# Lighter router and statistics, norms per tile, a fixed ring of contexts, two shared blocks in the transition, and text order from there on

## The chip, the cores and the metric

The kernel runs on one core of a Trainium2 chip. The metric is the device time of one execution in microseconds (us), the median of several runs; beside it stands one profiled execution, whose trace is what every reading here rests on. The engines are TensorE (PE, with its weight loads shown as PEld), VectorE (DVE), ScalarE (ACT), GpSimd (POOL) and SyncE (SP, which here issues DMAs).

## The reference

A block of cross attention is followed by a mixture of experts, all in fp32, on 32 sequences of 100 tokens with 256 features; each sequence has a context of 361 rows with 192 features.

```
x1 = layernorm(layernorm(x)); x2 = layernorm(ctx)           # affine forms of both
q, k, v = x1 Wq + bq, x2 Wk + bk, x2 Wv + bv                # E = 256, one head
x = x + softmax(q k^T / sqrt(E)) v Wo + bo
n = layernorm(x)
shared = gelu(n ws1 + bs1) ws2 + bs2                        # 256 -> 256 -> 256
aff = softmax(n Wr + br)                                    # 31 experts
gates = the 3 largest of aff, else 0
routed = sum over e of gates_e * (gelu(n We1_e + Be1_e) We2_e + Be2_e)
x = x + (shared + routed + n)
```

## The kernel before

The 3200 tokens are 25 tiles of 128, held in SBUF for the whole run as seven blocks `xb[k]` of up to four tiles. The work has four stages.

**Attention** loops over the 32 sequences (a batch each). Wq, Wk and Wv, Wo are folded into two matrices beforehand, so that one iteration transposes the context of batch i (`ctx_transpose`), computes the scores of batch i-1 (`scores`: the maximum on DVE, the exponential on ACT), and transposes and weighs batch i-2 (`exp_transpose`, `weighted`, which copies to a ring `cT`). When 128 tokens are done, `project_out` adds the result to the tile and takes its mean and variance. Contexts come in groups of GB = 4 batches: each has three chunks of rows, whose statistics are 12 `bn_stats` and 12 `bn_aggr`, followed by one `rsqrt` per group. That function is a root on ACT, a reciprocal on DVE and four DVE instructions of a Newton step; each root loads its own table on ACT, and so does the next exponential. The tile norms wait in the same way for `norms()`, once in four batches.

**Routing** is a pipeline through five functions of a tile, one step per iteration: `route_norm` normalises and transposes a tile, `route_gates` computes the logits, the three largest and a mask of the chosen experts, `route_slots` turns prefix counts (a running `base`, so that the tiles follow each other) into row numbers and scatters the tile's rows three times to `xs_d` in DRAM with indirect DMAs on POOL, `route_transpose` and `route_biases` add the gated second biases to the tile. POOL also adds the normalised tile to the tile itself (L500).

**The transition** derives from the counts which expert each of the 92 tiles of gathered rows belongs to, which takes a chain of small DVE instructions and a few transposes, and fetches rows and weights. The first shared block (`shared_first(0)`, `shared_second(0)`) is placed after it.

**The experts**: `run` handles 92 tiles; at step i it calls `turn(i)` (two transposes), `first(i-2)` (eight matmuls of We1, gelu on ACT) and `second(i-4)` (four matmuls of We2, a scaling, and a scatter to `y_d`). `fetch(q)` loads four tiles' rows and weights two groups ahead, `sort_out(q)` computes their gates and row numbers.

**The tail**: the other six shared blocks, and for each tile a read of its three rows from `y_d` (L929, four buffers), a sum on POOL (L931) and two on DVE (L932, L933), then one store per block.

A planner with a cost model orders the instructions of every engine; the text gives priorities and dependences. At run time each engine then works through its list in order, and each DMA queue its own.

Of the kernel before, what the change touches and what calls it, by code (L numbers as in the profile page):

```python
# [16 lines left out]
PSUM = bass.MemoryType.PSUM  # L17

# [16 lines left out]
def xattn_ffn(  # L35
# [27 lines left out]
    CODE, IX, GT, XW = D1, D1 + 1, D1 + 4, D1 + 8  # L63
    assert NS <= P and T % P == 0 and NE <= 32
# [14 lines left out]
    zpool = att_ctx.enter_context(tc.tile_pool(name="zpool", bufs=2 * GB + 2))  # L79
# [18 lines left out]

    ztile = {}

    def load_ctx(b):
        z = zpool.tile([P, NCH, DA], F32, tag="z", name=f"z_{b}")
        full = sum(1 for _, n in CH if n == P)
        nc.sync.dma_start(
            z[:, :full, :D2], ctx_in[b, : full * P, :].rearrange("(c p) d -> p c d", p=P)
        )
        for c in range(full, NCH):
            s, n = CH[c]
            nc.sync.dma_start(z[:n, c, :D2], ctx_in[b, s : s + n, :])
        nc.gpsimd.memset(z[:, :, D2:DA], 1.0)  # L110
        ztile[b] = z
# [35 lines left out]
    b2r = const.tile([NG, D1], F32, tag="b2r", name="b2r")  # L147
    nc.scalar.dma_start(b2r[:NE, :], Be2)
    nc.scalar.dma_start(b2r[NE:NG, :], bs2[None, :])
# [86 lines left out]
    for c in range(2):  # L236
# [6 lines left out]
        nc.vector.tensor_copy(m_sb[:, c, :], pm[:, :DA])  # L243
    AUG = [(0, 0, P), (1, P, A2)]
    c_sb = att.tile([P, 2], F32, tag="c", name="c_sb")
    for c, s, m in AUG:
# [6 lines left out]
        nc.vector.tensor_copy(c_sb[:m, c : c + 1], pc[:m, :1])  # L253
# [28 lines left out]
    def rsqrt(mv, n, mul, add, tag, name):  # L282

        v, s, y, r = (
            small.tile([P, n], F32, tag=f"{tag}{q}", name=f"{q}_{name}", bufs=3) for q in "vsyr"
        )
        nc.vector.tensor_scalar(v, mv[:, :, 1], mul, add, ALU.mult, ALU.add)
        nc.scalar.activation(s, v, AF.Sqrt)
        nc.vector.reciprocal(y, s)
        nc.vector.tensor_tensor(s, y, y, ALU.mult)  # L290
        nc.vector.tensor_tensor(s, s, v, ALU.mult)
        nc.vector.tensor_scalar(s, s, -0.5, 1.5, ALU.mult, ALU.add)
        nc.vector.tensor_tensor(r, y, s, ALU.mult)
        return r

# [3 lines left out]
    mvc, rc = {}, {}  # L299

    def ctx_stats_open(g):
        mvc[g] = small.tile([P, GB * NCH, 2], F32, tag="mvc", name=f"mvc_{g}", bufs=2)
        nc.gpsimd.memset(mvc[g], 1.0)

    def ctx_stats(b):
        g, i = divmod(b, GB)
        for c, (_, n) in enumerate(CH):
            stats(ztile[b][:n, c, :D2], mvc[g][:n, i * NCH + c, :], f"c{b}_{c}")

    def ctx_rsqrt(g):  # L310
        rc[g] = rsqrt(mvc[g], GB * NCH, 1.0, EPS, "c", f"c{g}")
# [8 lines left out]
    r1 = rsqrt(mv1, NT, 1.0 + EPS, EPS * EPS, "x", "x")  # L320
# [42 lines left out]
    def ctx_normalise(b):  # L363
        g, i = divmod(b, GB)
        z = ztile[b]
        for c, (_, n) in enumerate(CH):
            u = i * NCH + c
            normalise(z[:n, c, :D2], z[:n, c, :D2], mvc[g][:n, u, 0:1], rc[g][:n, u : u + 1])
# [14 lines left out]
    def scores(b):  # L383
# [7 lines left out]
        mx = small.tile([P, 1], F32, tag="mx", name=f"mx_{b}")  # L391
        nc.vector.tensor_reduce(mx[:L1, :], pss[:L1, :L2], AX.X, ALU.max)
        nm = small.tile([P, 1], F32, tag="nm", name=f"nm_{b}")
        nc.vector.tensor_scalar(nm[:L1, :], mx[:L1, :], -SC, None, ALU.mult)
        ex = work.tile([P, L2], F32, tag="ex", name=f"ex_{b}")
        nc.scalar.activation(ex[:L1, :], pss[:L1, :L2], AF.Exp, bias=nm[:L1, :], scale=SC)
# [16 lines left out]
    def weighted(b):  # L413
        z, exT = ztile.pop(b), att_eT.pop(b)
        for a, s, m in AUG:
# [6 lines left out]
            while q < L1:  # L422
                col = (b * L1 + q) % RING
                n = min(L1 - q, RING - col)
                if a == 0:
                    nc.scalar.copy(cT[:m, a, col : col + n], pw[:m, q : q + n])
                else:
                    nc.vector.tensor_copy(cT[:m, a, col : col + n], pw[:m, q : q + n])
# [3 lines left out]
    mv2 = {}  # L432

    def project_out(t, i, mv):
# [10 lines left out]
        stats(xt, mv[:, i, :], f"m{t}")  # L445

    xT = [qk[:, :, tiles[0] * P : (tiles[0] + len(tiles)) * P] for tiles in BLOCKS]
    GR = 4
    gates = const.tile([P, GR, NG], F32, tag="gates", name="gates")
    nc.gpsimd.memset(gates[:, :, NE:NG], 1.0)  # L450
# [43 lines left out]

    def route_norm(t):
# [4 lines left out]
        nc.gpsimd.tensor_tensor(xt, xt, xl, ALU.add)  # L500
        nc.gpsimd.tensor_scalar(row[:, CODE : CODE + 1], iota_3p, float(KTOP * P * t), None, ALU.add)
        nc.gpsimd.memset(row[:, XW - 1 : XW], 0.0)
# [6 lines left out]
    def route_gates(t):  # L509
# [16 lines left out]
        nc.vector.tensor_scalar(ix, i8[:, :KTOP], 1.0, None, ALU.add)  # L526
        mk = small.tile([P, NE], BF16, tag="mk", name=f"mk_{t}")
        nc.vector.tensor_scalar(mk, iota1, ix[:, 0:1], None, ALU.is_equal)
        for q in range(1, KTOP):
            nc.vector.scalar_tensor_tensor(mk, iota1, ix[:, q : q + 1], mk, ALU.is_equal, ALU.add)  # L530
# [4 lines left out]
        nc.vector.scalar_tensor_tensor(gates[:, t % GR, :NE], mk, rs, er, ALU.mult, ALU.mult)  # L535
        nc.scalar.activation(rows[t][:, GT : GT + KTOP], e3, AF.Copy, scale=rs)
        routing[t] = (mk, ix)

    def route_slots(t):

        mk, ix = routing.pop(t)
# [8 lines left out]
        sl = small.tile([P, KTOP], F32, tag="sl", name=f"sl_{t}")  # L550
        junk = small.tile([P, NE], F32, tag="junk", name=f"junk_{t}")
        for q in range(KTOP):
            nc.vector.scalar_tensor_tensor(
                junk, iota1, ix[:, q : q + 1], pos, ALU.is_equal, ALU.mult, accum_out=sl[:, q : q + 1]
            )
        su = small.tile([P, KTOP], U32, tag="su", name=f"su_{t}", bufs=6)
        nc.vector.tensor_copy(su, sl)
# [4 lines left out]
    def route_transpose(t):  # L562
        pg = ps_t(f"pg_{t}")
        nc.tensor.transpose(pg[:NG, :P], gates[:, t % GR, :], ident)
        gT[t] = small.tile([NG, P], F32, tag="gT", name=f"gT_{t}")
        nc.scalar.copy(gT[t], pg[:NG, :P])

    def route_biases(t):

        xt, _, _ = tile_of(t)  # L570
# [402 lines left out]
```

## Time and profile before

| | us |
|---|---|
| median of 3 runs | 577.51 (577.25 to 581.39) |
| profiled execution | 576.57 |
| its span, first to last instruction | 574.75 |
| last tile statistic of attention ends | 280.4 |
| last xs_d row numbers ready | 308.2 |
| first expert transpose | 325.26 |
| last expert scatter issued | 515.16 |
| first read of y_d issued | 520.22 |
| last DVE instruction ends | 568.91 |

| engine | busy us | share of the span |
|---|---|---|
| PE | 488.5 | 85% |
| DVE | 364.7 | 63% |
| ACT | 221.2 | 38% |
| POOL | 220.7 | 38% |

Busy shares are means over stages with different limits; a stage is read from its own window. The mean granted clock of PE is 0.918 of full speed. DMA moved 98.8 MB.

### The profile page before, as it was taken

The page shows a single profiled execution, that of the slowest core. Times are in us where ns is not written, and L with a number is a line of the kernel's source. Part 1 is how long each engine was busy: PE and PEld are TensorE (multiplying, and loading weights), DVE is VectorE, ACT ScalarE, POOL GpSimd, SP SyncE. Part 2 cuts the span into 40 slices and gives each one's busy share as a digit, 9 for nine tenths or more (in the row PEclk, how much of TensorE's full clock was granted, in tenths as well). Part 3 has the DMA queues.
Part 4 walks back from the last instruction along what each step waited for, and adds up shares of the span by engine and source line. Part 5 has one row for each costly group of instructions (what it writes and reads, how often), then busy time and mean ns, then how long its engine had stood idle before and what let it go on. Part 6 is the DMA issues. An engine that isn't in the chain of part 4 may idle for free. (4 is left out here: it accounts for less than half of the span.)

```text
span 574.8 us, 10701 instructions
## 1 busy us (share of the span) xinstructions
PE 488.5 (85%) x2798; PEld 387.9 (67%) x2798; DVE 364.7 (63%) x1737; ACT 221.2 (38%) x594; POOL 220.7 (38%) x334
## 2 busy tenths in 40 slices
PE   1649989888978979799665999999999999986892
PEld 1535757565656656577442699999999999973661
DVE  5497987997867989999876333433443343315663
ACT  0004463735426363736432244444444444431010
POOL 2000011443433344446675044444445444553432
PEclk9978988996968999999855899999999999999896
DMA  8892981221212131101222888888888888626975
GB/s 247 255 355 77 305 279 40 84 79 58 87 48 69 49 110 35 54 33 58 76 72 99 264 240 268 264 266 250 259 265 264 256 258 266 195 76 197 313 243 162
DMA packets 67634, 98.77 MB, mean 172 GB/s; under 512 B 8236, under 2 KB 43028, under 8 KB 67572
## 3 DMA queue, kind: packets, MB, share of 16 engines
q1 hardware_dynamic: 54880, 71.53, 41.9%
q0 software_dynamic: 8016, 22.21, 10.3%
q10 hardware_dynamic: 4676, 4.32, 2.3%
q8 instruction: 26, 0.43, 0.3%
q14 instruction: 36, 0.29, 0.2%
HBM read 68.22 MB, written 29.80 MB: 171 GB/s over the span
## 5 line engine op out<-in xcount | busy, mean ns | idle before, releaser
L456 POOL DMA_INDIRECT y_d<-ys,yrow x92 | 88.3, 959 | 115.2 <-DVE ys L874 72.5
L456 POOL DMA_INDIRECT xs_d<-xl,su x75 | 76.6, 1022 | 79.4 <-issue 14.8
L851 PE MATMUL ph<-xgT,w 128*128 128x128 f32 x736 | 101.6, 281 | 0.0
L856 ACT ACTIVATE hT<-ph,b1t 128x128 f32<-128x128 f32 x184 | 57.6, 364 | 101.7 <-PE ph L851 101.7
L851 PEld LDWEIGHTS ph<-xgT,w 128*128 128x128 f32 x736 | 94.8, 197 | 0.1
L866 PE MATMUL py<-w2r,hT 128*128 x368 | 94.3, 380 | 0.0
L866 PEld LDWEIGHTS py<-w2r,hT 128*128 128x128 f32 x368 | 62.9, 190 | 4.8
L418 PE MATMUL pcx<-exT,z 128*65 128x100 f32 (+3 forms) x384 | 50.9, 281 | 15.3 <-DVE exT L405 15.3
L418 PEld LDWEIGHTS pcx<-exT,z 128*65 128x65 f32 (+3 forms) x384 | 44.9, 175 | 24.1 <-DVE exT L405 22.5
L843 DVE COPY xgT<-pg 128x256 f32<-128x256 f32 x92 | 38.0, 418 | 34.1 <-PE pg L841 33.4
L387 PE MATMUL pss<-z2T,qk 65*100 65x361 f32 (+1 forms) x128 | 47.1, 488 | 0.4 <-DVE x L444 0.4
L874 DVE TENSOR_SCALAR ys<-py,gate 128x256 f32<-128x256 f32 x46 | 22.2, 482 | 37.0 <-PE py L866 37.0
L841 PEld LDWEIGHTS pg<-ident,xg 128*128 128x128 f32 x184 | 35.5, 197 | 5.2 <-DVE xgT L843 0.6
L822 DVE TENSOR_TENSOR eq<-xg,ebc 128x12 f32<-128x12 f32 x23 | 3.9, 171 | 51.4 <-DMA xg<-xs_d 51.4
L841 PE MATMUL pg<-ident,xg 128*128 128x128 f32 x184 | 36.1, 281 | 0.1
L297 DVE TENSOR_SCALAR z<-z,mvc,r_c 128x192 f32<-128x192 f32 (+1 forms) x96 | 33.7, 378 | 0.0
L931 POOL TENSOR_TENSOR y<-y 128x256 f32<-128x256 f32 x25 | 20.7, 829 | 31.6 <-DMA y<-y_d 29.4
L779 PE MATMUL pys<-ws_sb,hs 128*128 128x256 f32 x100 | 26.3, 412 | 7.1 <-DVE x L933 4.7
L279 DVE BATCH_NORM_STATS2 st_c<-z 128x6 f32<-128x192 f32 (+1 forms) x96 | 31.5, 338 | 0.0
L376 PE MATMUL pz<-ident,z 128*65 128x128 f32 (+2 forms) x192 | 29.4, 284 | 1.5 <-ACT qk L507 0.7
L439 PE MATMUL po<-wvo,cT 128*128 128x257 f32 (+1 forms) x100 | 30.3, 423 | 0.0
L779 PEld LDWEIGHTS pys<-ws_sb,hs 128*128 128x128 f32 x100 | 19.9, 204 | 15.0 <-ACT hs L772 9.6
(217 smaller groups left out, 880.0 us busy)
## 6 DMA issues: line engine op xcount, KB each, us to landing
w<-in_L_ffn_We_dram SPq DMA_DIRECT2D x92, 256.0 KB, 3.4
xg<-xs_d SPq DMA_DIRECT2D x92, 132.0 KB, 3.1
y<-y_d SPq DMA_DIRECT2D x25, 384.0 KB, 3.7
w2r<-in_L_ffn_We_dram SPq DMA_DIRECT2D x31, 256.0 KB, 5.6
z<-in_ctx_dram SPq DMA_DIRECT2D x32, 192.0 KB
xs_d<-none SPq DMA_DIRECT2D x3, 1056.0 KB
x<-in_x_dram SPq DMA_DIRECT2D x6, 512.0 KB, 3.6
out_dram<-x ACTq DMA_DIRECT2D x6, 512.0 KB, 6.2
```

Of the source, the lines that this page charges most:

```text
L279: nc.vector.bn_stats(st[:p, :], src)
L297: nc.vector.tensor_scalar(dst, src, mv, r, ALU.subtract, ALU.mult)
L387: nc.tensor.matmul(pss[:L1, :L2], qk[:m, a, b * L1 : (b + 1) * L1], z2T[:m, a, :], start=(a == 0), stop=(a == 1),)
L418: nc.tensor.matmul(pw[:m, :L1], z[:n, c, s : s + m], exT[:n, c, :], start=(c == 0), stop=(c == NCH - 1))
L439: nc.tensor.matmul(po[:, : D1 + 1], cT[:m, a, t * P % RING : t * P % RING + P], wvo[:m, a, :], start=(a == 0), stop=(a == 1))
L456: ins = nc.gpsimd.indirect_dma_start(out=dst, out_offset=bass.IndirectOffsetOnAxis(ap=index, axis=0), in_=src, in_offset=None).ins
L779: nc.tensor.matmul(py[:, :D1], h[:, f, j * P : (j + 1) * P], ws2_sb[:, f, :], start=(f == 0), stop=(f == 1))
L841: nc.tensor.transpose(pt[:, c * P : (c + 1) * P], g[:, c::2], ident)
L843: nc.vector.tensor_copy(xgT[i].rearrange("p c s -> p (c s)"), pt[:, : 2 * P])
L851: nc.tensor.matmul(ph[:, f * P : (f + 1) * P], w1s[:, c, f::2], z[:, c, :], start=(c == 0), stop=(c == 1))
L856: nc.scalar.activation(hT[i][:, f, :], ph[:, f * P : (f + 1) * P], AF.Gelu, bias=b1t[:, f, i : i + 1])
L866: nc.tensor.matmul(py[:, :D1], h[:, f, :], w2f[:, bass.ds(e * (2 * D1) + f * D1, D1)], start=(f == 0), stop=(f == 1),)
```

## The change

- **Statistics.** The contexts' `bn_aggr` is gone; POOL combines the two halves that `bn_stats` leaves and takes the inverse root there, as a power of -0.5 and one Newton step. Tokens get a root of their own per tile on POOL (`token_rsqrt`), one iteration before `route_norm` uses it; `norms()` is gone. The root on ACT is gone everywhere.
- **Scores.** The scale is folded into the projection, the maximum is negated as it is reduced, and both halves of `cT` are copied by ACT.
- **Router.** Mask and row numbers are each a comparison or product on 128 x 93 and a reduction. The gated biases leave the attention stage: the gates of a block are transposed at once, and `shared_second` has a third matmul per tile against a padded copy of the biases (`b2z`). The tile's sum with its normalised form becomes one DVE instruction (`residual`), for the first 8 tiles in `route_slots`, for the other 17 in the expert loop.
- **Contexts** lie in a fixed ring of ten buffers, whose constant column is written once.
- **Transition.** `shared_first(0)` stands before the selection chain, `shared_first(1)`, `shared_second(0)` and `shared_second(1)` behind it; five blocks are left for the tail.
- **Order.** From `shared_first(0)` to the end of the experts PE, DVE and ACT follow the text; in the tail POOL too. The tail has eleven buffers for y.

The diff, cut to its core:

```
+    ZB = 2 * GB + 2
+    zring = [att.tile([P, NCH, DA], F32, tag=f"z{q}", name=f"z{q}") for q in range(ZB)]
+    for z in zring:
+        nc.gpsimd.memset(z[:, :, D2:DA], 1.0)
     ztile = {}
     def load_ctx(b):
-        z = zpool.tile([P, NCH, DA], F32, tag="z", name=f"z_{b}")
+        z = zring[b % ZB]
         full = sum(1 for _, n in CH if n == P)
         nc.sync.dma_start(
             z[:, :full, :D2], ctx_in[b, : full * P, :].rearrange("(c p) d -> p c d", p=P)
@@ -107,7 +111,6 @@
         for c in range(full, NCH):
             s, n = CH[c]
             nc.sync.dma_start(z[:n, c, :D2], ctx_in[b, s : s + n, :])
-        nc.gpsimd.memset(z[:, :, D2:DA], 1.0)
         ztile[b] = z
...
-    b2r = const.tile([NG, D1], F32, tag="b2r", name="b2r")
-    nc.scalar.dma_start(b2r[:NE, :], Be2)
-    nc.scalar.dma_start(b2r[NE:NG, :], bs2[None, :])
+    b2z = const.tile([P, TPB, D1], F32, tag="b2z", name="b2z")
+    nc.gpsimd.memset(b2z, 0.0)
+    for j in range(TPB):
+        nc.scalar.dma_start(b2z[j * NG : j * NG + NE, j, :], Be2)
+        nc.scalar.dma_start(b2z[j * NG + NE : (j + 1) * NG, j, :], bs2[None, :])
...
-    def rsqrt(mv, n, mul, add, tag, name):
-        v, s, y, r = (
-            small.tile([P, n], F32, tag=f"{tag}{q}", name=f"{q}_{name}", bufs=3) for q in "vsyr"
-        )
-        nc.vector.tensor_scalar(v, mv[:, :, 1], mul, add, ALU.mult, ALU.add)
-        nc.scalar.activation(s, v, AF.Sqrt)
-        nc.vector.reciprocal(y, s)
-        nc.vector.tensor_tensor(s, y, y, ALU.mult)
-        nc.vector.tensor_tensor(s, s, v, ALU.mult)
-        nc.vector.tensor_scalar(s, s, -0.5, 1.5, ALU.mult, ALU.add)
-        nc.vector.tensor_tensor(r, y, s, ALU.mult)
+    mhalf = att.tile([P, NT], F32, tag="mhalf", name="mhalf")
+    nc.gpsimd.memset(mhalf, -0.5)
+    pool = nc.gpsimd
+    def small_t(n, tag, name, bufs=3):
+        return small.tile([P, n], F32, tag=tag, name=f"{tag}_{name}", bufs=bufs)
+    def rsqrt(v, n, tag, name, r=None):
+        y, s = (small_t(n, f"{tag}{q}", name) for q in "ys")
+        if r is None:
+            r = small_t(n, f"{tag}r", name)
+        pool.tensor_tensor(y, v, mhalf[:, :n], ALU.pow)
+        pool.tensor_tensor(s, y, y, ALU.mult)
+        pool.tensor_tensor(s, s, v, ALU.mult)
+        pool.tensor_scalar(s, s, -0.5, 1.5, ALU.mult, ALU.add)
+        pool.tensor_tensor(r, y, s, ALU.mult)
         return r
+    mv2 = const.tile([P, NT, 2], F32, tag="mv2", name="mv2")
+    r2 = const.tile([P, NT, 3], F32, tag="r2", name="r2")
+    def token_rsqrt(t):
+        v = small_t(1, "mv", f"m{t}")
+        pool.tensor_scalar(v, mv2[:, t, 1:2], EPS, None, ALU.add)
+        rsqrt(v, 1, "m", f"m{t}", r2[:, t, 0:1])
+        pool.tensor_scalar(r2[:, t, 1:2], r2[:, t, 0:1], 1.0, None, ALU.add)
+        pool.tensor_tensor(r2[:, t, 2:3], r2[:, t, 0:1], mv2[:, t, 0:1], ALU.mult)
...
-    mvc, rc = {}, {}
+    stc, mc, rc = {}, {}, {}
+    GC = GB * NCH
     def ctx_stats_open(g):
-        mvc[g] = small.tile([P, GB * NCH, 2], F32, tag="mvc", name=f"mvc_{g}", bufs=2)
-        nc.gpsimd.memset(mvc[g], 1.0)
+        stc[g] = small.tile([P, GC, 6], F32, tag="stc", name=f"stc_{g}", bufs=2)
+        pool.memset(stc[g], 1.0)
     def ctx_stats(b):
         g, i = divmod(b, GB)
         for c, (_, n) in enumerate(CH):
-            stats(ztile[b][:n, c, :D2], mvc[g][:n, i * NCH + c, :], f"c{b}_{c}")
+            nc.vector.bn_stats(stc[g][:n, i * NCH + c, :], ztile[b][:n, c, :D2])
     def ctx_rsqrt(g):
-        rc[g] = rsqrt(mvc[g], GB * NCH, 1.0, EPS, "c", f"c{g}")
+        s = stc[g]
+        h, q, v, m = (small_t(GC, f"c{w}", f"c{g}") for w in "hqvm")
+        pool.tensor_tensor(h, s[:, :, 1], s[:, :, 4], ALU.subtract)
+        pool.tensor_scalar(h, h, 0.5, None, ALU.mult)
+        pool.tensor_tensor(m, s[:, :, 4], h, ALU.add)
+        pool.tensor_tensor(q, s[:, :, 2], s[:, :, 5], ALU.add)
+        pool.tensor_scalar(q, q, 1.0 / D2, EPS, ALU.mult, ALU.add)
+        pool.tensor_tensor(h, h, h, ALU.mult)
+        pool.tensor_tensor(v, q, h, ALU.add)
+        mc[g], rc[g] = m, rsqrt(v, GC, "c", f"c{g}")
...
-        mx = small.tile([P, 1], F32, tag="mx", name=f"mx_{b}")
-        nc.vector.tensor_reduce(mx[:L1, :], pss[:L1, :L2], AX.X, ALU.max)
         nm = small.tile([P, 1], F32, tag="nm", name=f"nm_{b}")
-        nc.vector.tensor_scalar(nm[:L1, :], mx[:L1, :], -SC, None, ALU.mult)
+        nc.vector.tensor_reduce(nm[:L1, :], pss[:L1, :L2], AX.X, ALU.max, negate=True)
         ex = work.tile([P, L2], F32, tag="ex", name=f"ex_{b}")
-        nc.scalar.activation(ex[:L1, :], pss[:L1, :L2], AF.Exp, bias=nm[:L1, :], scale=SC)
+        nc.scalar.activation(ex[:L1, :], pss[:L1, :L2], AF.Exp, bias=nm[:L1, :])
...
-                if a == 0:
-                    nc.scalar.copy(cT[:m, a, col : col + n], pw[:m, q : q + n])
-                else:
-                    nc.vector.tensor_copy(cT[:m, a, col : col + n], pw[:m, q : q + n])
+                nc.scalar.copy(cT[:m, a, col : col + n], pw[:m, q : q + n])
...
+    def residual(t):
+        xt, _, _ = tile_of(t)
+        nc.vector.tensor_scalar(xt, xt, r2[:, t, 1:2], r2[:, t, 2:3], ALU.mult, ALU.subtract)
+    EARLY = 2
...
-        nc.gpsimd.tensor_tensor(xt, xt, xl, ALU.add)
         nc.gpsimd.tensor_scalar(row[:, CODE : CODE + 1], iota_3p, float(KTOP * P * t), None, ALU.add)
-        nc.gpsimd.memset(row[:, XW - 1 : XW], 0.0)
...
+        eq = small.tile([P, KTOP, NE], F32, tag="eq3", name=f"eq3_{t}", bufs=3)
+        nc.vector.tensor_tensor(
+            eq, iota1[:, None, :].to_broadcast([P, KTOP, NE]), ix[:, :, None].to_broadcast([P, KTOP, NE]),
+            ALU.is_equal,
+        )
         mk = small.tile([P, NE], BF16, tag="mk", name=f"mk_{t}")
-        nc.vector.tensor_scalar(mk, iota1, ix[:, 0:1], None, ALU.is_equal)
-        for q in range(1, KTOP):
-            nc.vector.scalar_tensor_tensor(mk, iota1, ix[:, q : q + 1], mk, ALU.is_equal, ALU.add)
+        nc.vector.tensor_reduce(mk, eq.rearrange("p k e -> p e k"), AX.X, ALU.max)
...
-        sl = small.tile([P, KTOP], F32, tag="sl", name=f"sl_{t}")
-        junk = small.tile([P, NE], F32, tag="junk", name=f"junk_{t}")
-        for q in range(KTOP):
-            nc.vector.scalar_tensor_tensor(
-                junk, iota1, ix[:, q : q + 1], pos, ALU.is_equal, ALU.mult, accum_out=sl[:, q : q + 1]
-            )
+        nc.vector.tensor_tensor(eq, eq, pos[:, None, :].to_broadcast([P, KTOP, NE]), ALU.mult)
         su = small.tile([P, KTOP], U32, tag="su", name=f"su_{t}", bufs=6)
-        nc.vector.tensor_copy(su, sl)
+        nc.vector.tensor_reduce(su, eq, AX.X, ALU.max)
+        if t // TPB < EARLY:
+            residual(t)
...
-        pg = ps_t(f"pg_{t}")
-        nc.tensor.transpose(pg[:NG, :P], gates[:, t % GR, :], ident)
-        gT[t] = small.tile([NG, P], F32, tag="gT", name=f"gT_{t}")
-        nc.scalar.copy(gT[t], pg[:NG, :P])
-    def route_biases(t):
-        xt, _, _ = tile_of(t)
-        pb = ps_m(f"pbb_{t}")
-        nc.tensor.matmul(pb[:, :D1], gT.pop(t), b2r, start=True, stop=True)
-        nc.vector.tensor_tensor(xt, pb[:, :D1], xt, ALU.add)
-    ROUTE = (route_norm, route_gates, route_slots, route_transpose, route_biases)
+        k, j = divmod(t, TPB)
+        if j + 1 == len(BLOCKS[k]):
+            pg = ps_t(f"pg_{t}")
+            nc.tensor.transpose(pg[:, :P], gates[:, k % 2, :, :].rearrange("p j e -> p (j e)"), ident)
+            gT[k] = const.tile([P, P], F32, tag=f"gT{k}", name=f"gT_{k}")
+            nc.scalar.copy(gT[k], pg[:, :P])
+    ROUTE = (route_norm, route_gates, route_slots, route_transpose)
...
+            project_out(done_t)
+            token_rsqrt(done_t)
+            norm2[done_t] = (mv2[:, done_t, 0:1], r2[:, done_t, 0:1])
...
+        route_step()
         outputs((i - 2) * L1)
-        route_step()
...
+            nc.tensor.matmul(py[:, :D1], gT[k], b2z[:, j, :], start=False, stop=True)
...
     while norm2 or routed:
         route_step()
+    in_order = ExitStack()
+    in_order.enter_context(tc.manual_schedule(engines={ET.PE, ET.DVE, ET.Activation}))
+    shared_first(0)
...
-    def run(first_, last_, between=()):
+    def run(first_, last_):
         qs = range(first_ // GM, (last_ + GM - 1) // GM)
-        fetch(qs[0])
-        if len(qs) > 1:
-            fetch(qs[1])
-        for f in between:
-            f()
-        sort_out(qs[0])
         for i in range(first_, last_ + SECOND):
             q = i // GM
             if i % GM == 0 and q + 2 in qs:
                 fetch(q + 2)
-            if i % GM == 1 and q + 1 in qs:
+            if i == first_ + 3:
+                sort_out(q)
+            if i % GM == 3 and q + 1 in qs:
                 sort_out(q + 1)
+            if first_ == 0 and i % GM == 1 and q + EARLY * TPB < NT:
+                residual(q + EARLY * TPB)
...
-    total = []
-    run(0, NU, (
-        lambda: shared_first(0), lambda: total.append(registers()), lambda: shared_second(0),
-    ))
-    with tc.If(total[0] > NU):
+    fetch(0)
+    fetch(1)
+    shared_first(1)
+    total = registers()
+    shared_second(0)
+    shared_second(1)
+    run(0, NU)
+    in_order.close()
+    with tc.If(total > NU):
+        fetch(NU // GM)
+        fetch(NU // GM + 1)
         run(NU, NS)
-    for k in range(1, len(BLOCKS)):
-        shared_first(k)
-        shared_second(k)
...
+    ypool = ctx.enter_context(tc.tile_pool(name="ypool", bufs=11, reuse_waits="tile"))
+    y3s = {}
+    def collect(t):
+        y3 = y3s[t] = ypool.tile([P, KTOP, D1], F32, tag="y3", name=f"y3_{t}")
+        reads("y", nc.sync.dma_start(y3.rearrange("p k d -> p (k d)"), yv[t]))
+    def total_of(k):
+        tiles = BLOCKS[k]
         for j, t in enumerate(tiles):
-            y3 = hpool.tile([P, KTOP, D1], F32, tag="y3", name=f"y3_{t}", bufs=4)
-            reads("y", nc.sync.dma_start(y3.rearrange("p k d -> p (k d)"), yv[t]))
-            xt = xb[k][:, j, :]
+            y3, xt = y3s.pop(t), xb[k][:, j, :]
...
+    LAST = len(BLOCKS) - 1
+    for t in (*BLOCKS[0], *BLOCKS[1]):
+        collect(t)
+    with tc.manual_schedule(engines={ET.PE, ET.DVE, ET.Activation, ET.Pool}):
+        shared_first(EARLY)
+        for k in range(EARLY, LAST + 1):
+            if k < LAST:
+                shared_first(k + 1)
+            if k > EARLY:
+                store(k - EARLY - 1)
+            shared_second(k)
+            total_of(k - EARLY)
+            for t in BLOCKS[k]:
+                collect(t)
+        store(LAST - EARLY)
+        for k in range(LAST - EARLY + 1, LAST + 1):
+            total_of(k)
+            store(k)
```

## The prediction

> **What bounds the kernel now.** I read the busy times of the span in stages first, then each engine's groups of instructions inside the attention stage, the waits, the timeline where the stages meet, and the chain of waits at the end. Busy time by stage (window and its length, then busy us of PE, PE's weight loads, DVE, ACT and POOL, the granted clock, the DMA share, GB/s):
>
> ```profile
> 40.00:280.00 240.00, 212.99 (x1217) 152.44 (x1218) 207.70 (x1074) 118.74 (x309) 83.53 (x150) 0.92 0.29 94
> 280.00:325.26 45.26, 30.08 (x94) 17.02 (x93) 28.85 (x184) 13.91 (x41) 24.16 (x31) 0.59 0.38 123
> 325.26:514.00 188.74, 188.32 (x1288) 178.34 (x1288) 72.29 (x288) 79.25 (x230) 86.44 (x91) 1.00 0.81 243
> 514.00:574.75 60.75, 41.02 (x132) 26.32 (x132) 31.60 (x71) 7.59 (x13) 22.50 (x27) 0.87 0.69 223
> ```
>
> Attention (40 to 280) has two nearly full engines, PE with 213.0 and DVE with 207.7 of 240 us; PE is idle for 27.0. The transition (280 to 325) fills nothing: it is a chain. The expert stage is PE without a gap at full clock, 92 tiles of 2.04 us. The tail has a DMA share of 0.69. What DVE and PE do in attention that the change touches, and whom PE waits for:
>
> ```profile
> L553 DVE SCALAR_TENSOR_TENSOR junk<-iota,xl,pos 128x31 f32<-128x31 f32 x57 | 14.0, 246 | 0.0
> L280 DVE BATCH_NORM_AGGREGATE mvc<-st_c 128x2 f32<-128x6 f32 (+1 forms) x84 | 13.4, 166 | 0.0
> ...
> L428 DVE COPY cT<-pcx 65x100 f32<-65x100 f32 (+8 forms) x36 | 8.4, 242 | 8.2 <-PE pcx L418 7.6 <-PE pp L544 0.3
> ```
>
> ```profile
> L572 PE MATMUL pbb<-b2r,gT 32*128 32x256 f32 x36 | 13.0, 441 | 1.5 <-DVE cT L428 0.7 <-DVE s_m L291 0.7
> ...
> L564 PE MATMUL pg<-ident,gates 128*32 128x128 f32 x19 | 5.5, 289 | 2.8 <-DVE z2T L380 2.8
> ```
>
> ```profile
> PE pcx L418 <- DVE exT L405: 15.3, 16, 2.6
> ```
>
> A group's columns are busy us, mean ns of one, and the idle time before it with its releasers; a wait's are us in total, times, longest. Of the 27.0 us that PE is idle, 15.3 is PE waiting for a copy out of DVE's long queue.
>
> **Attention, DVE.** Neighbouring DVE instructions overlap by about 0.07 us (a 0.33 us statistic started at 33.62, the next instruction at 33.87), so I count mean less 0.07. Removed: the 84 aggregates of the contexts, 84 x 0.096 = 8.1; 32 scalings of the maximum (L394, 0.141), 2.3; 36 copies of cT, moved to ACT, 6.2, and the 8.2 idle before them; 18 bias adds (L573, 0.42), 6.3 and 1.5 idle; the arithmetic of rsqrt (L287 to L293, 14.7 us in 88 instructions), 8.5. The router's ten instructions per tile (L528, L530, L553 with its reads, L557: 35.9 us in 19 tiles) cost 1.4 a tile after overlap; their four successors on 128x93 have no row. A 128x12 TENSOR_TENSOR is 0.171 (L822), a 128x256 one 0.41 (L932), so 0.25 each by a straight line, 0.72 a tile after overlap; bounds 0.4 and 1.36. That is 12.9 less. Eight residuals come in at 0.35, 2.8. Sum: 41.5 busy and 9.7 idle; DVE falls from 207.7 to 166.
>
> **Attention, PE.** 18 bias matmuls (13.0) leave, and 14 of 19 gate transposes (4.1): 213.0 to 196. DVE then has slack, and I let 10 of the 27 idle go, two thirds of the 15.3. The stage becomes 196 + 17 = 213, a gain of **27**. Bounds: 8, if only about half of the removed PE work shows because new waits eat the rest; 44, if all idle time goes. ACT takes the cT copies (36 x 0.24 = 8.7) and drops 14 root tables with most of the 15 loads that bring the exponential back, each 1.28; it is busy for 118.7 of 240, so both cost or save nothing unless a table stands before an exponential that PE needs. The extra six loads of b2z on ACT's queue (0.25 to 0.32 each) lie ahead of ACT's first work at 34.4, after the last load at 15.5; z's constant column, set once, takes 32 memsets off POOL, which waited 38.1 us for z's readers.
>
> **Attention, POOL.** This is the new price. POOL today scatters three times a tile, one every 1.26 us (0.96 and 0.30 of issue), 3.8 a tile. It gains 8 small instructions per tile and 13 per four batches (4.2 a tile), and loses the 0.75 us add and two kinds of memset. With the one it keeps, that is 13 small ones; the timeline (start us, us, then what ran)
>
> ```profile
> 268.58 0.22 POOL L501 TENSOR_SCALAR xl<-iota_3p 128x1 f32<-128x1 f32 x1
> 268.84 0.10 POOL L502 MEMSET xl<- 128x1 f32 x1
> ...
> 293.41 1.41 POOL L500 TENSOR_TENSOR x<-x,xl 128x256 f32<-128x256 f32 x2
> ...
> 293.59 0.63 DVE L553 SCALAR_TENSOR_TENSOR junk<-iota,xl,pos 128x31 f32<-128x31 f32 x1
> ```
>
> gives 0.26 from one to the next, 3.4 a tile, 7.2 in all. The new pace is 213 / 25 = 8.5 us a tile, so POOL fits at 85%. The power has no row: from below 0.22 (L501), from above 1.02 (the scatter, POOL's dearest); I take it as a small instruction, 0.26, and the upper end adds 1.0 a tile, 8.2, which still fits. Queued behind a power or a scatter on POOL are the next tile's root and, behind that on DVE, the normalisation, now a whole step later than its statistic, which is some 6 us of cover.
>
> The rows also show a two-input DVE instruction of usually 0.246 us taking 0.63 under two adds of POOL. The Trainium skill, page "SBUF — State Buffer", section "Who interferes with whom", calls the read and write pair that DVE and GpSimd share an exclusive lock: a two-input DVE instruction and a reading GpSimd instruction block each other for their full length. If by that rule each of the 13 x 25 small instructions held DVE for its 0.26 us, an estimate, DVE would gain 84 us, stand at 250, and the stage would be longer than before. The rows do not ask for that: most of DVE's time goes to instructions that read one operand or PSUM, and the sum has nothing for it.
>
> **The transition.** After the last statistic (280.2) six tiles still have to be placed, one every 4.3 us:
>
> ```profile
> 300.17 0.19 PE L543 MATMUL pp<-mk,before 128*128 128x31 bf16 x1 [1.77 <-DVE mk L530]
> ...
> 302.52 0.42 DVE L573 TENSOR_TENSOR x<-pbb,x 128x256 f32<-128x256 f32 x1 [0.76 <-PE pbb L572]
> ...
> 304.45 0.18 PE L543 MATMUL pp<-mk,before 128*128 128x31 bf16 x1 [1.72 <-DVE mk L530]
> ...
> 315.05 6.00 PE L769 MATMUL phs<-qk,ws_sb 128*128 128x512 f32 x8
> ```
>
> The last slot is written at 308.2, 28 us on. With a root per tile only tiles 22, 23 and 24 are left, and a step loses the wait of 0.76 and the add of 0.42: three steps of 3.2 make 10. Gain 18. From there to the first expert transpose took 17.1. Now the first shared product runs under the selection chain (at most 1.5 of delay for the transposes behind it on PE): p_b ends 6.9 + 1.5 later, the second product takes 6.0, and two second halves follow. Each has 24 instead of 16 matmuls, because the biases ride in them: 3.8 x 1.5 = 5.7. With 0.5 for the registers, 26.3, so 9.2 is given back. Net gain **8.8**, bounds 0 and 12. The scattered rows land some 24 us after the last slot by the same spacings and are hidden behind this.
>
> **The expert stage.** PE keeps its 14 matmuls a tile in the order that the trace has, so 0. Residuals (17 x 0.35) and the later sort of rows lie in DVE's idle 60%; uncovered, they would cost 6.
>
> **The tail.** PE begins at 515.7 as before. Five first halves instead of six: 4 x 3.6 + 1.1 = 15.5; five second halves: 4 x 5.7 + 1.7 = 24.5. PE ends at 555.7. The sums of tiles 16 to 24 follow on DVE, nine pairs at about 0.75, so 562.6; from the last DVE end to the end of the span it was 5.9 (568.9 to 574.75). 568.5 is a gain of **6.3**. Eleven buffers instead of four let the reads run ahead: 520.2 is their start, and 13.1 MB at the best 5 us rate of the tail, 370 GB/s, take 35, so 12 is the upper bound; the lower is 0, if DVE, now in text order, waits for a read with PE's adds behind it.
>
> **The sum.** The profiled execution took 576.57, its span 574.75 and 1.8 around it, and lies 0.94 under the median of the runs. 576.57 - 27 - 8.8 - 6.3 = 534.5, and with the 0.9 about **535**.
>
> **Rivals.** (1) *In-order stalls keep attention near its old length*: DVE now waits for POOL 33 times (25 tiles, 8 groups), and POOL may stand behind three scatters, 3.8 us. No wait of DVE for POOL is in the trace, but POOL is busy for only 35% of this stage, so that is no proof. At 0.8 us a time it costs 26: 562; I span 557 to 575. (2) *POOL becomes the bound, slower than before*: place, the power on POOL. Routing started near 85 us, so 25 tiles at a POOL time of T end at 85 + 25 T, experts start 27 later, and the tail returns 6. This equals today's 325 + 6 at T = 8.8, that is a power of about 1.5 us, 1.3 of them per tile. At 2 us, T = 9.5: 595. For: no row shows this operation. Against: 1.5 is above POOL's dearest row, 1.02. (3) *Both queues fall into step*: attention gains 44, transition 12, tail 12: 509.
>
> **How the numbers follow.** The forecast has 0.62 with its own range of 515 to 557; (3) 0.07; (1) 0.20, of which 0.05 lies within 1% of the median (571.7 to 583.3, about what a measurement of this kernel tells from no change); (2) 0.11. Faster: 0.62 + 0.07 + 0.15 = 0.84. The range, 509 to 565, leaves out 0.11 above from (2) and part of (1) and a little below.
>
> **What would show it.** Right: no root table on ACT; PE over 90% busy in a stage of 205 to 220 us; the first expert transpose near 289; experts at 2.04 us a tile; the tail's PE without a gap over 2 us. Wrong: a power of over 1.5 us, waits of DVE for POOL of over 15 us in all, or first expert matmuls later than 310.

## The result and the profile after

The changed kernel takes 605.35 us (median of four, 604.28 to 606.88), the kernel before 577.38 on the same chips: a ratio of 1.0476, 95% interval 1.0416 to 1.0537. It is **slower by 4.8%**, where 535 was forecast. (All ratios below are against the kernel before on the same chip and leave out executions that were slowed at a lower granted clock, such as two of the four with idle chains and one of the four of the fastest kernel, so a ratio is not always the quotient of two medians.)

The busy times by stage of the changed kernel, cut where its last token statistic (324.6), its first expert transpose (361) and the end of the experts (549) lie; columns as before (window, length, then busy us of PE, weight loads, DVE, ACT, POOL, granted clock, DMA share, GB/s):

```profile
40.00:325.00 285.00, 215.25 (x1199) 159.97 (x1199) 180.75 (x766) 89.73 (x304) 158.21 (x387) 0.84 0.30 90
325.00:361.00 36.00, 26.23 (x90) 17.32 (x91) 14.53 (x76) 7.68 (x20) 13.12 (x24) 0.77 0.46 149
361.00:549.00 188.00, 187.55 (x1289) 178.11 (x1287) 83.49 (x317) 79.06 (x230) 86.28 (x90) 1.00 0.80 238
549.00:604.30 55.30, 36.93 (x142) 26.53 (x142) 31.51 (x67) 6.43 (x11) 21.23 (x27) 0.88 0.73 245
```

Attention is 285 us long instead of 240, though DVE has only 180.8 us of work in it for more tiles than the 207.7 of before. No engine is full any more: PE 76%, DVE 63%, POOL 56%. Such a stage is bound by a chain, and the waits name it (us in total, times, longest):

```profile
DVE xl L319 <- POOL r L304: 64.1, 25, 8.2
...
PE pcx L451 <- DVE exT L438: 31.2, 19, 5.6
...
PE pl L538 <- DVE xl L319: 25.3, 12, 7.5
...
DVE z L319 <- POOL cr_c L304: 18.4, 6, 4.6
```

DVE, which did not wait for POOL in this stage before, now waits for the token root at every one of the 25 tiles, for a context root at six of eight groups, and once (3.2 us) for the root of x: 85.7 us. Behind the waiting normalisation stand the copies that PE needs, so PE's wait for the copy exT has doubled from 15.3 to 31.2. One of these waits, in the timeline of DVE (start us, us, what ran, and the idle time before it):

```profile
237.34 0.17 DVE L286 BATCH_NORM_AGGREGATE mv<-st_m 128x2 f32<-128x6 f32 x1
237.43 0.50 DVE L415 COPY z2T<-pz 65x361 f32<-65x361 f32 x1
237.85 0.24 DVE L570 SCALAR_TENSOR_TENSOR gates<-mk,rs,er 128x31 f32<-128x31 bf16 x1
238.01 0.35 DVE L438 COPY exT<-pe 128x200 f32<-128x200 f32 x1
238.28 0.52 DVE L427 TENSOR_REDUCE nm<-pss 100x1 f32<-100x361 f32 x1
238.72 0.37 DVE L319 TENSOR_SCALAR z<-z,cm_c,cr_c 105x192 f32<-105x192 f32 x1
241.37 0.41 DVE L319 TENSOR_SCALAR xl<-x,mv,r 128x256 f32<-128x256 f32 x1 [2.28 <-POOL r L304]
```

and the same moment on POOL:

```profile
238.32 0.96 POOL L483 DMA_INDIRECT xs_d<-xl,su  x1 [0.30 <-issue]
239.35 0.24 POOL L313 TENSOR_SCALAR mv_m<-mv 128x1 f32<-128x1 f32 x1
239.68 0.57 POOL L300 TENSOR_TENSOR my_m<-mv_m,mhalf 128x1 f32<-128x1 f32 x1
240.32 0.19 POOL L301 TENSOR_TENSOR ms_m<-my_m 128x1 f32<-128x1 f32 x1
...
241.15 0.19 POOL L304 TENSOR_TENSOR r<-my_m,ms_m 128x1 f32<-128x1 f32 x1
```

The statistic ends at 237.51. POOL is still scattering and takes it up 1.84 us after that; the six instructions up to the root need 1.99 more; DVE has five other instructions up to 239.09, and then the normalisation is next in its order, with ready work queued behind it. Over the 25 tiles the queue on POOL is 1.88 us and the chain 2.16; the normalisation starts as soon as the root is there, 4.07 us after the statistic, of which DVE has work for 1.5. In the order as built the normalisation is on average the fifth DVE instruction after its tile's statistic (5.3 places); before, with norms in batches, it was about the 97th (the 29th at the least). The text puts a step between the two; the planner, which orders DVE here, has moved the normalisation forward. A context root has no shorter way: it comes on average 7.8 us after the last statistic of its group, 6.2 of them the chain of twelve instructions.

### The profile page after: what moved, and what is told of

Read it like the earlier page. It is cut to its first block, busy times and chain, and to the rows that moved or that the text cites. A ratio compares the mean times of both kernels' runs of the same rounds, so it can differ in the third digit from the quotient of the medians.

```text
span 604.3 us, 10397 instructions
## 1 busy us (share of the span) xinstructions
PE 483.0 (80%) x2780; PEld 396.1 (66%) x2780; DVE 331.5 (55%) x1321; ACT 182.9 (30%) x564; POOL 287.6 (48%) x566
## 5 line engine op out<-in xcount | busy, mean ns | idle before, releaser
L451 PE MATMUL pcx<-exT,z 128*65 128x100 f32 (+3 forms) x384 | 51.7, 289 | 31.3 <-DVE exT L438 31.2
L319 DVE TENSOR_SCALAR xl<-x,mv,r 128x256 f32<-128x256 f32 x25 | 10.5, 420 | 64.1 <-POOL r L304 64.1
L319 DVE TENSOR_SCALAR z<-z,cm_c,cr_c 128x192 f32<-128x192 f32 (+1 forms) x96 | 33.6, 376 | 18.4 <-POOL cr_c L304 18.4
L538 PE MATMUL pl<-ident,xl 128*128 128x128 f32 x50 | 14.2, 369 | 33.9 <-DVE xl L319 25.3
L411 PE MATMUL pz<-ident,z 128*128 128x128 f32 (+2 forms) x192 | 32.1, 306 | 3.3 <-DVE z L319 3.3
L538 PEld LDWEIGHTS pl<-ident,xl 128*128 128x128 f32 x50 | 8.4, 215 | 38.6 <-DVE xl L319 22.8
L467 PE MATMUL po<-wvo,cT 128*128 128x257 f32 (+1 forms) x100 | 33.0, 455 | 0.0
L411 PEld LDWEIGHTS pz<-ident,z 128*128 128x128 f32 (+2 forms) x192 | 27.2, 165 | 7.8 <-DVE z L319 3.7
L963 POOL TENSOR_TENSOR y<-y 128x256 f32<-128x256 f32 x25 | 19.3, 772 | 24.3 <-DMA y<-y_d 22.4
```

The source lines that it names most:

```text
L319: nc.vector.tensor_scalar(dst, src, mv, r, ALU.subtract, ALU.mult)
L411: nc.tensor.transpose(pt[:m, ks : ks + n], z[:n, c, s : s + m], ident[:n, :n])
L451: nc.tensor.matmul(pw[:m, :L1], z[:n, c, s : s + m], exT[:n, c, :], start=(c == 0), stop=(c == NCH - 1))
L467: nc.tensor.matmul(po[:, : D1 + 1], cT[:m, a, t * P % RING : t * P % RING + P], wvo[:m, a, :], start=(a == 0), stop=(a == 1))
L538: nc.tensor.transpose(pt[:, c * P : (c + 1) * P], xl[:, c::2], ident)
```

## The experiments

The theory (A): the roots are *late*, and DVE stands in order behind them. Rivals: (B) POOL has too much work, or its work slows DVE; (C) another part of the change is to blame. Last slot is the start of the last su in the trace; waits are DVE's for POOL between 30 us and the experts.

| kernel | waits, us | last slot, us | median, us | ratio [95%] |
|---|---|---|---|---|
| before | 0 | 308.2 | 577.4 | 1 |
| changed | 85.7 | 334.8 | 605.4 | 1.048 [1.042, 1.054] |
| all roots on DVE and ACT | 0 | 289.0 | 563.8 | 0.975 [0.969, 0.981] |
| token roots there | 24.6 | 314.6 | 586.8 | 1.013 [1.005, 1.020] |
| context roots and x there | 46.2 | 304.8 | 579.6 | 1.002 [0.998, 1.006] |
| router a step later | 51.8 | 313.8 | 591.0 | 1.021 [1.014, 1.028] |
| router two steps later | 58.2 | 319.4 | 591.2 | 1.028 [1.022, 1.035] |
| no Newton step | 49.0 | 310.8 | 582.8 | 1.003 [0.996, 1.010] |
| first roots on DVE | 76.6 | 329.3 | 599.9 | 1.042 [1.035, 1.049] |
| contexts on DVE, router a step later | 25.0 | 278.7 | 550.6 | 0.957 [0.951, 0.962] |
| the same, no Newton step for tokens | 9.7 | 257.9 | 531.6 | 0.924 [0.917, 0.932] |
| all roots on DVE and ACT, idle chains on POOL | 0 | 294.4 | 565.5 | 0.963 [0.952, 0.975] |
| all roots as logarithm and exponential on ACT | 0 (70.7 for ACT) | 374.9 | 647.0 | 1.110 [1.101, 1.119] |
| before, its roots on POOL | 32.5 | 335.0 | 603.4 | 1.036 [1.028, 1.044] |

**All roots off POOL.** In the changed kernel, in short:

```
-        pool.tensor_tensor(y, v, mhalf[:, :n], ALU.pow)
+        nc.scalar.activation(s, v, AF.Sqrt)
+        nc.vector.reciprocal(y, s)
...     (and pool. becomes nc.vector. in rsqrt, token_rsqrt, ctx_rsqrt and v1)
```

> All roots (tokens, contexts, x) leave POOL: the small arithmetic runs on DVE and the root itself is a square root on ACT with a reciprocal on DVE, one per tile. The rest of the change stays. Theory A (DVE stands in order behind POOL's chain for the root, 33 waits of 82.5 us in all, since only about 5 instructions lie between a statistic and its normalisation on DVE): the waits of DVE for POOL vanish; DVE gets about 300 small instructions of some 0.1 us net, 30 us, and ACT 33 roots with two table loads of 1.28 each, of which a part stalls an exponential; so 545 to 570. Theory B (POOL is the bound by its own work): POOL loses about 75 us of work, so the same 545 to 570. Theory C (another part of the change, or the order that it brings, is to blame): 595 or more, with other waits in their place.

563.8 us, ratio 0.975: 0.072 less than the changed kernel, some 42 us. The waits are gone, the last slot is 46 us earlier, and the rest of the change is therefore worth a gain of 2.5% (against C), even with up to two table loads for each root:

```profile
L302 ACT ACT_TABLE_LOAD x29 | 37.2, 1283 | 23.4 <-DMA z<-in_ctx_dram 22.9
L434 ACT ACT_TABLE_LOAD x21 | 26.9, 1283 | 0.4
...
L559 ACT ACT_TABLE_LOAD x8 | 10.3, 1283 | 0.1
```

**Each half alone.** The same edit for the tokens only, and for the contexts and x only.

> Only the roots of the token tiles leave POOL (square root on ACT, arithmetic on DVE); contexts and x keep theirs on POOL. A: the 64 us of xl's waits vanish and the 18 us of the contexts' stay; DVE gets 200 small instructions, about 20 us: 555 to 580. B: POOL loses some 2.1 us a tile, also 555 to 580. C: 595 or more.

> Only the roots of the contexts and of x leave POOL; the token tiles keep theirs there. A: only the 18 us of z's waits vanish, and tokens wait a little less since no context chain stands ahead of theirs: 580 to 598. B: POOL loses 8 chains of about 5.5 us, 44 us in all, as much as the 25 token chains hold, so as large a gain as from these: 560 to 580. C: 600 or more.

Tokens: 586.8, 7 us beyond the forecast's end: xl's 64 us of waiting are gone, but 46 table loads (59 us of ACT) have come; whether they make the difference was not tried. Contexts: 579.6. This one gave more than forecast under A, because xl's waits fell with z's, from 64.1 to 46.2: the context chain had stood ahead of the token chains on POOL, whose wait there before they start falls from 1.88 to 1.28 us a tile. Of 39.5 us of waiting removed, 26 show in the time. By themselves these runs fit B as well as A.

**More cover, POOL's work untouched.** In short:

```
-            norm2[done_t] = (mv2[:, done_t, 0:1], r2[:, done_t, 0:1])
+            fresh_norms.append(done_t)      # handed to norm2 after the next route_step
```

> POOL keeps all its work; only the text hands a tile to the router one step later, which leaves on average 16 instead of 5 DVE instructions between a tile's statistic and its normalisation. A: cover grows from about 1.5 to about 5 us a tile, the waits of xl fall from 64 to 20 to 35 us, and one step more is needed at the end of the stage: 565 to 585. B: POOL's work is the same, so 600 to 606. C: no forecast of a gain, 600 to 610.

591.0: some 15 us less with POOL busier than before the edit (293.5 against 287.6 us), so B is contradicted, and so is C. xl's waits fall to 29.9, as A said, but the time gains less than it forecast: the contexts' 18.7 stay, the cover of 5.3 us on average is uneven (0.7 to 14.4), and the planner again placed the normalisation only 3 to 10 instructions behind the statistic for twelve of the tiles.

> All roots on POOL as in the changed kernel, a tile handed to the router two steps later: 31 DVE instructions on average between statistic and normalisation (16 with one step, 5 in the changed kernel), though the planner leaves only 3 to 16 for the first five tiles and the last five. A: the waits of xl fall from 64 to 10 to 20 us, those of the contexts (18) stay, and the last tile is placed a step later, 5 to 8 us: 578 to 592. B: POOL's work is unchanged, 600 or more.

591.2, no further gain: xl still waits 27.2 and the contexts 27.8, 9 us more than with one step, and the last statistic comes 6 us later (305.9 against 299.6). A later place in the text alone does not cure it while the context chains are on POOL too.

**POOL's work without the waiting.** All roots on DVE and ACT, and on POOL the same chains again for nobody, in short:

```
+    def idle_chain(src, n, tag, name, pre):
+        for _ in range(pre): pool.tensor_scalar(h, src, 1.0, 1.0, ALU.mult, ALU.add)
+        pool.tensor_tensor(y, h, mhalf[:, :n], ALU.pow)
+        for _ in range(3): pool.tensor_tensor(y, y, h, ALU.mult)
+        pool.tensor_scalar(y, y, -0.5, 1.5, ALU.mult, ALU.add)
```

> The roots stand on DVE and ACT as in the run with all roots off POOL, and POOL besides runs chains of the same number, kind and size as the changed kernel's (33 chains and that of x, with their powers) on the same statistics, whose results nobody reads. A (it is the waiting that costs): the same as that run, ratio to before 0.97 to 0.985, 560 to 570. B (POOL's amount of work is the bound) and the variant that POOL's work slows DVE at a shared port: POOL is as full as in the changed kernel, so 590 or more.

565.5 us (556.8 to 568.6), ratio 0.963 [0.952, 0.975], no worse than without the chains (0.975 [0.969, 0.981]), and the longest of its four executions lies 21 us below what B asked for. POOL is as busy (287.4 us) as in the changed kernel (287.6), also from 40 us to the last slot (165.0 against 166.0), though a tile's idle chain has seven instructions and not eight. This is the run that settles it: neither the amount of POOL's work nor its neighbourhood costs anything that this can measure; somebody waiting for it does.

**The chain made shorter.** The power alone is the root; the Newton step is left out:

```
-        pool.tensor_tensor(s, y, y, ALU.mult)
-        pool.tensor_tensor(s, s, v, ALU.mult)
-        pool.tensor_scalar(s, s, -0.5, 1.5, ALU.mult, ALU.add)
-        pool.tensor_tensor(r, y, s, ALU.mult)
```

> The changed kernel with the four instructions of the Newton step left out of every chain, so that the power itself is the root; all roots stay on POOL. A: each root is ready 4 x 0.28 = 1.1 us sooner, and DVE waits 25 + 8 + 1 times for one: up to 37 us less, some of it lost where POOL itself waits; 575 to 590. B: POOL loses about 30 us of its 158 in the stage, and a bound POOL would give all of it back: 575. If neither holds (C): 600 or more.

582.8. A token's chain is 0.92 us instead of 2.16, xl waits 23.3 instead of 64.1, and all waits fall by 36.7, where up to 37 was forecast; the contexts wait a little longer, 23.7 for 18.4. Some 26 us of time go with four instructions of about 0.2 us in each chain. POOL also has 24 us of work less (263.7 us), so by itself this run does not tell A from B.

**A late root on another engine.** Roots off POOL as in the first run, with

```
-            nc.scalar.activation(s, v, AF.Sqrt)
-            e.reciprocal(y, s)
+            nc.scalar.activation(s, v, AF.Ln)
+            nc.scalar.activation(y, s, AF.Exp, scale=-0.5)
```

> As the run with all roots on DVE and ACT, but the root is an exponential of minus half a logarithm on ACT, so that ACT may keep one table instead of bringing two for each root (58 loads of 1.28 us in that run). A: if the loads fall away, 75 us of ACT's work go and some stalls of exponentials with them: 545 to 560. If a table is still brought for each, 560 to 575.

647.0, ratio 1.110 [1.101, 1.119], far outside both forecasts. The table loads did not fall away, they grew from 58 to 67, and nearly all stand two inside a root:

```profile
L302 ACT ACT_TABLE_LOAD x34 | 43.6, 1283 | 25.2 <-DMA z<-in_ctx_dram 24.6
L303 ACT ACT_TABLE_LOAD x33 | 42.3, 1283 | 0.6
```

```profile
DVE ms_m L306 <- ACT my_m L303: 52.2, 24, 4.3
...
DVE cs_c L306 <- ACT cy_c L303: 18.5, 8, 3.0
```

The mechanism is the same: DVE waits 70.7 us for roots, now from ACT. With the square root a token's variance is back from ACT after 1.5 us, and DVE has work for 2.4 before it needs it; here it comes after 3.2, and the built order has work for 1.2. The Trainium skill, page "ScalarE: Activation LUTs", section "Table sets: the hidden batching unit", counts one load for a logarithm followed by an exponential, since one set holds both. This run disagrees: 67 loads on these two lines for 34 roots, so a set with both cannot have stayed loaded.

**The kernel before, with its roots on POOL.** `rsqrt` of before in POOL's instructions (power and Newton step), batches as they were.

> The kernel before, with its root arithmetic moved to POOL (power and Newton step there) and nothing else changed: its norms stay in batches of three or four tiles, and on average 70 DVE instructions lie between a tile's last statistic and its normalisation. A: with that cover tokens don't wait; the contexts' groups, whose normalisation follows soon, wait some 2 to 4 us eight times, and the first ones late by the 4 us power; DVE loses about 12 us of work: 570 to 592. B or a dear POOL by itself: POOL gets only some 40 us more of work, also 570 to 592. C (what else was changed is to blame): 575 or less.

603.4, ratio 1.036 [1.028, 1.044], above the forecast. Its DVE waits:

```profile
DVE z L300 <- POOL z L110: 15.6, 5, 3.9
DVE z L300 <- POOL r_c L296: 10.3, 3, 4.0
...
DVE xl L300 <- POOL r_m L296: 3.8, 4, 2.3
```

With some 78 DVE instructions between statistic and normalisation the tokens wait for 3.8 us in all instead of 64.1, as A says of cover. The first line names a memset of z's constant column, but z does not wait for it; at one of the five places

```profile
88.42 0.21 POOL L296 TENSOR_TENSOR r_c<-y_c,s_c 128x12 f32<-128x12 f32 x1
88.58 0.10 POOL L110 MEMSET z<- 128x3 f32 x1
88.67 0.38 DVE L300 TENSOR_SCALAR z<-z,mvc,r_c 128x192 f32<-128x192 f32 x1 [3.00 <-POOL z L110]
```

z starts 0.04 us after the end of the root and before the memset ends. So both lines are the wait for a context's root, 25.9 us in all, one of 2.3 to 4.0 us for each of the eight groups, as A forecast; with 2.5 for the root of x and 4.1 for the tokens (0.3 of them under the memset's name as well) it is 32.5, against 23 us of lost time. The move of the roots to POOL is thus a loss by itself, without any other part of the change, and here it comes mainly from the context roots, for which DVE waits in both kernels.

**Where the start goes, and both remedies.**

> The changed kernel with only the very first roots off POOL: those of x and of the first four contexts stand on DVE and ACT, all others on POOL. In the changed kernel the first normalisation of a context starts at 47.7 us, with these roots off POOL and all later context roots too at 44.6, and the first row is placed at 104.5 against 87.8. If the 4.4 us and 2.3 us powers at the start set that loss of 16.7 us, the first row is placed before 93 and the time falls by 10 to 15: 590 to 596. If the later groups' chains make it, only some 3 to 5 us come back: 598 to 603.

The first row is placed at 92.6 instead of 104.5, so the two chains at the start, with powers of 4.4 and 2.3 us, make 11.9 of the 16.7 us; yet the time is 599.9, for 61.3 of xl's 64.1 us stay and half of the 12 us is given back by the last slot (329.3 against 334.8). The early reading was right for the place and wrong for the time.

> Contexts and x have their roots on DVE and ACT, the tokens theirs on POOL, handed to the router one step later: both remedies, each in part. A: the waits of xl fall from 46 (contexts on DVE alone) to 10 to 20 us; half of the difference shows, less a step at the end: 563 to 575. B: 579 as with the contexts on DVE alone.

> As the run with contexts on DVE and tokens one step later on POOL, and without the four instructions of the Newton step in the token chains on POOL. A: a token root is ready 1.1 us sooner, up to 10 waits of that are left to shorten: 555 to 570, with DVE 12 us of work lighter than where all roots are on it, so it may match that run (563.8).

550.6 and 531.6 (530.4 to 544.4), both well below the forecasts. In the first a token's root comes 4.1 us after its statistic, against 5.1 with the step alone, and DVE has work for 5.4 on average, though twelve tiles still wait. Together the two remedies give 0.091 of the time before, alone 0.046 and 0.027. The waits do not explain this surplus: they fall by 60.7 us together, alone by 39.5 and 33.9. Its cause stays open. Both beat both kernels, the first with all of the arithmetic, the second without the Newton step of the token roots. In the second the waits and the attention stage are

```profile
DVE xl L325 <- POOL r L305: 9.7, 7, 2.7
```

```profile
40.00:245.30 205.30, 186.48 (x1182) 142.96 (x1182) 182.09 (x831) 105.44 (x320) 100.99 (x182) 0.96 0.39 123
```

## Why the prediction was wrong

**The step that failed** is in the POOL part: the normalisation is "now a whole step later than its statistic, which is some 6 us of cover". On it rests that the sum has no term for waiting. I read the cover out of the text, but the planner sets DVE's order in this stage, and the built order left 5 instructions, 1.5 us. With 6 us at every tile nearly all of the tokens' 64.1 us would have been hidden, an estimate: the root comes 4.04 us after the statistic on average, and only three of 25 come later than 6, by 8.3 us together. For the context groups the step is missing: their 13 instructions are in the sum as POOL's work, not as a delay, and DVE waited 18.4 us for their roots and 3.2 for that of x. In time they weigh as much: contexts and x off POOL gave back 26 us, the tokens alone 20, both together 42. The stage, from 40 to the last statistic, went from 240.2 to 284.6, 44 longer instead of 27 shorter; that is the whole error.

**Rival (1) named the mechanism** and mis-sized its price: "33 times at 0.8 us" was 32 times at 2.7. "No wait of DVE for POOL is in the trace" was right for attention only; in the tail of the kernel before there are six (`DVE x L933 <- POOL y L931: 3.4, 6, 0.6`). My 0.8 had no row behind it, and POOL's low busy share is no measure of it: a root that finds POOL free still takes 2. Rival (2), POOL as the bound through the power, did not happen: POOL is busy for 56%, and a token's power is 0.58 us, under the 1.02 of the upper end. What I had not priced is the power on wide tiles, here the groups of POOL:

```profile
L300 POOL TENSOR_TENSOR cy_c<-cv_c,mhalf 128x12 f32<-128x12 f32 x8 | 18.4, 2303 | 0.5
L300 POOL TENSOR_TENSOR my_m<-mv_m,mhalf 128x1 f32<-128x1 f32 x25 | 14.5, 578 | 1.9
...
L304 POOL TENSOR_TENSOR r<-my_m,ms_m 128x1 f32<-128x1 f32 x25 | 4.7, 190 | 1.9
L300 POOL TENSOR_TENSOR xy_x<-xv_x,mhalf 128x25 f32<-128x25 f32 x1 | 4.4, 4368 | 0.1
```

**DVE's term of work was right, PE's was not.** DVE did 186.0 us from 40 to the last slot against 229.0 before, 43.0 less (41.5 forecast for the shorter stretch to the last statistic). One part of that sum is off: ten router instructions with an overlap of 0.07 each are 1.2 us a tile and not 1.4, some 4 us in 19 tiles. The new ones, estimated at 0.25 each, came out. Below is a two-input one in the changed kernel, then with all roots on DVE and ACT, then with the idle chains besides:

```profile
L585 DVE TENSOR_TENSOR eq<-eq,pos 128x93 f32<-128x93 f32 x25 | 6.5, 261 | 0.0
...
L590 DVE TENSOR_TENSOR eq<-eq,pos 128x93 f32<-128x93 f32 x25 | 6.3, 251 | 0.0
...
L603 DVE TENSOR_TENSOR eq<-eq,pos 128x93 f32<-128x93 f32 x25 | 6.4, 255 | 0.0
```

The last two, 251 and 255 ns with POOL's work doubled, and DVE's work up to the last slot in the same two runs, 208.3 and 208.7 us, are the answer on the lock of the page "SBUF — State Buffer" that the prediction weighed: 84 us by its estimate, 0.4 us here for POOL's instructions of this size; leaving it out of the sum was right. (Beside an add of POOL on 128x256 a DVE add of 0.42 us takes 0.95, at 588.43 in the changed kernel, so large tiles do show such an effect.) ACT has no root table left (two loads in the whole run), as forecast. PE was busy for 215.3 us in the stage where 196 was forecast, at a granted clock of 0.84 for 0.92 before, though 64 of its 1277 matmul records up to the last slot are gone. The work removed paid only once the roots came in time: in the last run above the stage is 205.3 us with PE 91% busy (186.5 us, clock 0.96), and the first expert copy starts at 286.1. These are the marks that the forecast had set for itself, 205 to 220, over 90%, and 289, though that kernel has the context roots on DVE and ACT and no Newton step for tokens.

**Transition, experts and tail.** From the last statistic to the last slot 10.2 us (10 forecast), from there to the first expert transpose 26.1 (26.3): a net gain of 8.8, as forecast. The experts take as long as before, within 0.5 us. The tail, from the last scatter to the end, is 54.0 instead of 59.6, a gain of 5.6 for 6.3, but by two errors that cancel. A second half takes PE 5.2 us and not 5.7, so PE's tail is 36.9 us for 40; DVE's sums end 13 us after it, not 6.9, since the text order keeps the sums of 13 tiles, not of nine, behind all of PE's work, and they run from 586 to 600 one after another. In all 8.8 + 5.6 + 0.5 = 14.9 come back of the 44.4 lost: 29.5, the growth of the span from 574.75 to 604.3.

**The wrong-signs** that the prediction listed did fire: waits of DVE for POOL over 15 us (85.7), the first expert work after 310 (361), and a power of over 1.5 us, though on the wide tiles alone (2.30 and 4.37). Faster had 0.84; the chance of 0.11 for slower rested on the power's price alone, which left out that waits of the same kind as rival (1)'s could be long enough to lose.

## What to carry to other kernels

When arithmetic moves to an idle engine, price the time from its input to its output there, queue included, against the instructions that the consumer's engine has *in the built order* between the two; neither the idle share of the engine nor the distance in the text says it. Here a root that came 4 us after its input, with 1.5 us of cover, cost more than its removal from a nearly full engine gave, and the tokens' roots with cover were nearly free (some 4 us of waiting). Test it by running the moved work for nobody: if that costs nothing, the cure is cover or a shorter chain, not less work.

## What the hardware showed unexpectedly

A power on POOL grows with the tile, 0.58 us for 1 column, 2.30 for 12 and 4.37 for 25, which is about 0.42 us and 0.16 for each column, while the other small instructions of POOL take 0.19 to 0.28 us from 1 to 25 columns. Dependent ones of one column start 0.28 us apart (240.32, 240.60, 240.87 and 241.15 in the timeline above).

PE's busy time for about the same matmuls (1213 and 1208 records) from 40 us to the last slot is 219.0 us in the changed kernel, at a granted clock of 0.83, and 192.2 in the fastest run, at 0.93. Waits that leave PE idle thus go with slower matmuls too; whether the idleness causes the lower clock was not tried.
